# One core, two layers: the weight pieces beside the attention get a tile for their taps, loaded one piece ahead, and a second ring for their rows

## The chip, the core and the metric

The kernel runs on one NeuronCore of a Trainium2 chip. The metric is the device time of one execution in microseconds (us): the median over several executions. The core has five engines that each work through their own list of instructions in order: TensorE (PE in the profile, with its weight loads as PEld), VectorE (DVE), ScalarE (ACT), GpSimd (POOL) and SyncE (SP), which here only issues DMA transfers. They meet at semaphores.

## What is computed

The input is `x`, 4 images of 512 channels by 32 by 32. Two layers follow each other, each with a residual sum. The first is a group norm and a selective-scan (Mamba) layer; it is untouched here. The second, cut to what matters:

```python
x = x + L1(_gn(x))
def L1(x):                                   # per image: 512 channels, 32*32 = 1024 places
    top, center = conv1x1(x, w_top), conv1x1(x, w_center)     # 64 channels each
    bottom = conv3x3(x, w_bottom)                             # 512 channels
    sp = softmax(center.T @ top)                              # over all 1024*1024 entries
    y = (sp @ bottom).reshape(c, h, w)
    return conv3x3(x + y, w_out)
```

All arithmetic is in float32.

## The kernel before

**The two 3x3 convolutions** (`conv3`, lines 1428 to 1524) are done in a transformed form: a convolution's output is put together from 24 products, one for each of six row combinations `p` and four column combinations `q`. So the weights have to be transformed once: from nine taps to 6 x 4 matrices of 512 by 512. These lie in device memory, four tensors `u_b` (for `w_bottom`) and four `u_o` (for `w_out`). For each product `conv3` loads 1 MB of them into a tile `uw` (line 1479, ring `u`, three tiles), issues eight passes of 128x512 matmuls for it (line 1483), and the sums go through DVE and POOL. The inputs of a product come from `spread` (four DVE instructions into a tile `v`, ring `v`, two tiles), which reads a row pair `rr` (`row_pair`, line 1384: a ring `rr` with one single tile). A pair is made from temporaries `e`, `f`, `g`, `h`, `k`, `l` (ring `rt`, four tiles): `e` and `f` start on ACT (line 1393), the rest is POOL work.

**The weight transform** is cut into 16 pieces per weight (128 input channels by 128 output channels, all taps). All of `w_bottom` and the first two pieces of `w_out` are done during the first layer. The other 14 pieces of `w_out` are done in the second layer by `piece` (lines 1400 to 1426), beside the attention of the images 0 and 1, seven each. A piece before the change: load the three tap rows (192 KB each, lines 1408 to 1410) into a tile of the ring `v`, in which six rows stand; combine the taps to rows in place (six DVE instructions, lines 1414 to 1419, 128x384 elements each); combine the columns of all six rows at once into a tile `wo` of the ring `u` (three DVE instructions, lines 1422 to 1424, 128x768 each); store four results of 384 KB, two straight from the tile `w`, two from `wo` (line 1426).

**The order of the second layer** (lines 1604 to 1626). For images 0 and 1: `scores` (the two 1x1 convolutions `pt`, sixteen score matmuls `psc`, each copied from PSUM to `st` by ACT at line 1349, then exponentials), `conv3` with `u_b`, `attend`, and at the end `conv3` with `u_o` for both. `attend` (lines 1526 to 1552) has eight steps. Each is eight accumulating products into a PSUM tile `pat` (line 1533), which DVE then adds to the image `xg` (line 1546). After that of steps 1 to 7 one `piece` is called. PSUM tiles of `pat`, `pt` and `psc` share a ring `ps` of three. `attend` of image 0 is followed by `scores` and `conv3` of image 1, `attend` of image 1 by `conv3` of image 0 with `u_o`, which needs every piece.

The order within each engine is set by a scheduler that sorts the program's instructions by priority as it places them and gives out ring tiles; a tile is given again only when all its readers are through, DMAs too. So the order on an engine isn't exactly that of the text. The order on TensorE is the same before and after the change. On the other engines it moves near the pieces; where the prediction uses such a place it says so.

Of the kernel before, what the change touches and what calls it, by code (L numbers as in the profile page):

```python
# [8 lines left out]
F32 = mybir.dt.float32  # L9
AF = mybir.ActivationFunctionType  # L10
ALU = mybir.AluOpType
# [4 lines left out]
P = 128  # L16
B, C, HH, WW = 4, 512, 32, 32
L = HH * WW
NCC = C // P
# [150 lines left out]
def mamba_then_pab_kernel(  # L170
# [25 lines left out]
    nc = tc.nc  # L196
# [24 lines left out]
    for name, src in (("b", b_bottom), ("o", b_out)):  # L221
        t = cpool.tile([1, C], F32, tag=f"brow_{name}", name=f"brow_{name}")
# [6 lines left out]
    def padded(b, pool, tag):  # L229
# [44 lines left out]
    with ExitStack() as l0:  # L274
# [9 lines left out]
        QC = C // 4  # L284
# [933 lines left out]
        for k in range(NPC + EARLY):  # L1218
            u, src = ((ub, w_bottom), (uo, w_out))[k // NPC]
# [8 lines left out]
        for b in range(B):  # L1228
            at = b * NDC * NS
            for n in range(NDC):  # L1230
# [14 lines left out]
                y = [buf(f"y{j}", [P, NK, P], f"y_{b}_{n}_{j}") for j in range(2)]  # L1245
# [14 lines left out]
    with ExitStack() as l1:  # L1260
# [105 lines left out]
        shape = [P, NCC, TI, WW + 2]  # L1366
# [19 lines left out]
        def first_inputs(name, xg):  # L1386

            r = row_pair(name, 1)
            ts = []
            for n, a in (("e", 2), ("f", 1)):  # L1390
                t = tmp(n, name)
                rows = [xg[:, :, k : k + 4 * TI - 3 : 4, :] for k in (a, a + 2)]
                nc.scalar.activation(t, rows[0], AF.Copy, scale=-4.0)
                nc.gpsimd.tensor_add(t, t, rows[1])
                ts.append(t)
            nc.vector.tensor_add(r[:, 0], *ts)
            nc.vector.tensor_sub(r[:, 1], *ts)
            return spread(name, 1, r)

        def piece(k):  # L1400

            c, part = divmod(k, C // QC)
            cs = slice(part * QC, (part + 1) * QC)
            taps = w_out[c * P : (c + 1) * P, :, cs].rearrange("p (y x) o -> p y x o", y=3)
            t = xp.tile([P, NQ, 2, NCC, P], F32, tag="v", name=f"w_{k}", bufs=2)
            t = t.rearrange("p q n c t -> p (q n c t)").rearrange("p (r o) -> p r o", o=QC)
            g, mid = (t[:, a : a + n].rearrange("p (r x) o -> p r x o", x=3) for a, n in ((0, 3 * NP6), (3 * NP6, 3)))
            nc.sync.dma_start(g[:, 0], taps[:, 0])
            nc.sync.dma_start(g[:, NP6 - 1], taps[:, 2])
            nc.sync.dma_start(mid[:, 0], taps[:, 1])  # L1410
            r = [g[:, n].rearrange("p x o -> p (x o)") for n in range(NP6)]
            m = mid[:, 0].rearrange("p x o -> p (x o)")
            stt, dve = nc.vector.scalar_tensor_tensor, nc.vector
            dve.tensor_add(r[1], r[0], r[5])
            stt(r[3], r[5], 4.0, r[0], ALU.mult, ALU.add)
            dve.tensor_sub(r[2], r[1], m)
            dve.tensor_add(r[1], r[1], m)
            stt(r[4], m, -2.0, r[3], ALU.mult, ALU.add)
            stt(r[3], m, 2.0, r[3], ALU.mult, ALU.add)
            o = fp.tile([P, NCC, C], F32, tag="u", name=f"wo_{k}", bufs=3)  # L1420
            o = o.rearrange("p c o -> p (c o)").rearrange("p (q r o) -> p q r o", o=QC, r=8)[:, :, :NP6]
            dve.tensor_add(o[:, 0], g[:, :, 0], g[:, :, 2])
            dve.tensor_sub(o[:, 1], o[:, 0], g[:, :, 1])
            dve.tensor_add(o[:, 0], o[:, 0], g[:, :, 1])
            for q, part in enumerate((g[:, :, 0], o[:, 0], o[:, 1], g[:, :, 2])):
                nc.sync.dma_start(uo[q].rearrange("n p c o -> p n c o")[:, :, c, cs], part)

        def conv3(name, xg, u, bias, first=None, late=None, mid=None):

# [95 lines left out]

        def attend(b, xg, st, rp, xb, between, also):


            for k in range(NCC * NH):
                j, h = divmod(k, NH)  # L1530
                pt = ps.tile([P, C], F32, tag="ps", name=f"pat_{b}_{j}_{h}")
                for m in range(NMC):
                    nc.tensor.matmul(  # L1533
                        pt, st[m][:, 2 * P * j + h : 2 * P * (j + 1) : 2],
                        xb[m // 2][:, m % 2, :],
                        start=(m == 0), stop=(m == NMC - 1),
                    )
                if k == 0:
                    pz = ps.tile([P, T], F32, tag="ps", name=f"pz_{b}")
                    nc.tensor.matmul(pz[:, 0:1], ones, rp, start=True, stop=True)  # L1540
                    rz = spool.tile([P, 1], F32, tag="rz", name=f"rz_{b}")
                    nc.vector.reciprocal(rz, pz[:, 0:1])
                    for _ in between:
                        pass
                img = xg[:, j, 1 + h * HR : 1 + (h + 1) * HR, 1 : WW + 1]
                nc.vector.scalar_tensor_tensor(
                    img, pt.rearrange("p (h w) -> p h w", w=WW), rz, img,
                    ALU.mult, ALU.add,
                )
                for job in also[k : k + 1]:  # L1550
                    if job is not None:
                        piece(job)

        dst = [out[b].rearrange("(c p) h w -> p c (h w)", p=P) for b in range(B)]

# [47 lines left out]

        left = list(range(EARLY, NPC))
        half = len(left) // 2
        st, rp = scores(0, image[0])
        for a in range(0, B, 2):
            for b in (a, a + 1):
                xb = conv3(f"b{b}", image[b], ub, brow[0])
                also = [None] * (8 - half) + left[b * half : (b + 1) * half] if not a else []  # L1610
                after, v = iter(()), None
                if b == a:
                    after = norm(b + 1)
                    next(after)
# [69 lines left out]
```

## Time and profile before

| | |
|---|---|
| median of 3 runs | 3077.31 us (3075.14 to 3077.47) |
| profiled execution, its own time | 3080.41 us |
| span from first to last instruction in it | 3078.6 us |
| mean granted TensorE clock | 0.967 |
| busy: PE, DVE, ACT, POOL | 89%, 78%, 60%, 66% |
| DMA moved | 610.47 MB, mean 198 GB/s |

The profiled execution is 3.1 us (0.1%) longer than the median, and its own time is 1.8 us longer than its span. Times inside it are counted from the start of the span. The first layer takes the first two thirds; the attention of image 0 stands at about 2120 to 2176 us, that of image 1 at about 2296 to 2351 us. In the rows of the timeline the columns are start, time taken, engine, line and operation, output and inputs, count, and in brackets the idle time just before with what ended it. TensorE runs a float32 product in two passes, so counts of matmuls are twice those of the text.

### The profile page before, as it was taken

How to read it: one execution, taken by the hardware profiler on the slowest of the kernel's cores; microseconds unless marked ns; L12 is line 12 of the kernel's file. 1: busy time of each engine (PE TensorE's matmuls, PEld its weight loads, DVE VectorE, ACT ScalarE, POOL GpSimd, SP SyncE). 2: the span in 40 equal slices, each digit the busy share in tenths (PEclk: the TensorE clock that was granted, in tenths of full speed). 3: DMA queues.
4: the chain of work that ended last, by engine and by line, in shares of the span. 5: the costliest groups of instructions: out<-in, count | busy, mean ns of one | idle time of the engine just before them, and what ended most of it. 6: DMA issues, size and time to landing. Idle time of an engine off the chain costs nothing.

```text
span 3078.6 us, 35834 instructions
## 1 busy us (share of the span) xinstructions
PE 2745.6 (89%) x11512; PEld 1611.2 (52%) x11512; DVE 2395.5 (78%) x3129; ACT 1842.3 (60%) x3179; POOL 2022.4 (66%) x1047
## 2 busy tenths in 40 slices
PE   4789789999889999889999978799895999999998
PEld 2346556666666656556666655544342444444444
DVE  3569999989999989999999999976756475456164
ACT  4579889998789999789999888530210012130000
POOL 7899977899967889967989999743230332233132
PEclk9899899999999999999999999999997999999999
DMA  6766544577734567734667754566776897718397
GB/s 182 205 193 206 167 119 141 166 214 230 223 111 144 165 194 237 234 105 138 176 181 215 220 158 147 134 218 232 232 259 190 290 329 248 286 55 286 126 318 259
DMA packets 408500, 610.47 MB, mean 198 GB/s; under 512 B 46041, under 2 KB 244953, under 8 KB 383737
## 3 DMA queue, kind: packets, MB, share of 16 engines
q1 hardware_dynamic: 399504, 593.66, 61.3%
q10 hardware_dynamic: 8648, 14.26, 1.3%
q8 instruction: 92, 1.51, 0.2%
q14 instruction: 96, 0.78, 0.1%
q0 software_dynamic: 160, 0.26, 0.0%
HBM read 511.09 MB, written 96.99 MB: 198 GB/s over the span
## 4 chain that ended last, share of the span: by engine, by line
PE 42%; DVE 22%; ACT 12%; DMA 5%; issue 5%; POOL 4%; SPq 0%; DVEq 0%; POOLq 0%; ACTq 0%
PE m_b L1483 10%; PE m_o L1483 10%; DVE da L884 7%; PE y L913 4%; PE pat L1533 4%; DVE u L884 3%; ACT sc L844 3%; PE pz L394 2%; DVE dbx L884 2%; PE po L394 2%; PE u L870 2%; ACT da L832 2%; PE psc L1345 2%; ACT u L832 2%; DVE dbx L900 2%
## 5 line engine op out<-in xcount | busy, mean ns | idle before, releaser
L906 POOL TENSOR_TENSOR da<-da,cbc 128x1024 f32<-128x1024 f32 x288 | 680.8, 2369 | 154.6 <-DVE carry_sb L889 63.9
L859 POOL TENSOR_TENSOR dbx<-dtx,bbc 128x1024 f32<-128x1024 f32 x224 | 530.0, 2371 | 59.6 <-PE y L913 32.2
L844 ACT ACTIVATE sc<-dtxt,bt_sb 128x256 f32<-128x256 f32 x1152 | 504.7, 497 | 48.2 <-PE u L870 47.6
L832 ACT ACTIVATE da<-dt,a_sb 128x512 f32<-128x512 f32 x576 | 395.0, 713 | 39.7 <-PE y L913 34.3
L884 DVE TENSOR_TENSOR_SCAN da<-da,carry_sb,u 128x512 f32<-128x512 f32 x288 | 356.0, 1262 | 27.7 <-PE u L870 22.3
L913 PE MATMUL y<-ident,da 128*128 128x128 f32 x2304 | 319.9, 282 | 56.4 <-POOL da L906 52.6
L1483 PE MATMUL m_o<-uw_o,v_o 128*128 128x512 f32 x768 | 337.9, 600 | 35.8 <-DMA uw_o<-u_o 35.8
L870 PE MATMUL u<-ident,sc 128*128 128x128 f32 x2304 | 335.7, 278 | 38.0 <-DVE da L884 28.1
L884 DVE TENSOR_TENSOR_SCAN da<-da,u 128x512 f32<-128x512 f32 x288 | 348.7, 1211 | 3.9 <-PE u L870 3.6
L913 PEld LDWEIGHTS y<-ident,da 128*128 128x128 f32 x2304 | 268.4, 145 | 159.0 <-POOL da L906 107.5
L1483 PE MATMUL m_b<-uw_b,v_b 128*128 128x512 f32 x768 | 336.5, 598 | 7.4 <-DMA uw_b<-u_b 7.4
L870 PEld LDWEIGHTS u<-ident,sc 128*128 128x128 f32 x2304 | 268.5, 143 | 113.9 <-DVE da L884 38.7
L832 ACT ACTIVATE u<-dt,a_sb 128x512 f32<-128x512 f32 x448 | 297.4, 681 | 37.3 <-DVE dbx L900 14.7
L913 PE MATMUL y<-ident,dbx 128*128 128x128 f32 x1792 | 255.8, 281 | 23.8 <-POOL dbx L906 14.0
L394 PE MATMUL pxm<-xt,winc 128*128 128x345 f32 (+3 forms) x704 | 252.5, 501 | 27.3 <-DMA winc<-in_w_in_dram 12.6
L913 PEld LDWEIGHTS y<-ident,dbx 128*128 128x128 f32 x1792 | 209.8, 144 | 100.5 <-issue 32.1
L1483 PEld LDWEIGHTS m_o<-uw_o,v_o 128*128 128x128 f32 x768 | 146.3, 192 | 219.7 <-issue 180.6
L394 PE MATMUL pz<-xt,winc 128*128 128x512 f32 x512 | 242.3, 600 | 11.5 <-ACT sz L707 2.1
L1483 PEld LDWEIGHTS m_b<-uw_b,v_b 128*128 128x128 f32 x768 | 146.1, 191 | 193.5 <-issue 183.4
L906 POOL TENSOR_TENSOR dbx<-dbx,cbc 128x1024 f32<-128x1024 f32 x96 | 227.1, 2366 | 26.1 <-DVE carry_sb L889 17.2
L1533 PE MATMUL pat<-y_b,st 128*128 128x512 f32 x512 | 221.6, 593 | 0.4 <-ACT grstd_l L255 0.4
L394 PEld LDWEIGHTS pxm<-xt,winc 128*128 128x128 f32 x704 | 132.7, 199 | 116.0 <-issue 49.1
(232 smaller groups left out, 4316.8 us busy)
## 6 DMA issues: line engine op xcount, KB each, us to landing
cbc<-bcd SPq DMA_DIRECT2D x512, 256.0 KB, 3.7
uw_b<-u_b SPq DMA_DIRECT2D x96, 1024.0 KB, 4.8
uw_o<-u_o SPq DMA_DIRECT2D x96, 1024.0 KB, 4.8
bbc<-bcd SPq DMA_DIRECT2D x224, 256.0 KB, 3.6
u_b<-work SPq DMA_DIRECT2D x192, 128.0 KB, 2.7
winc<-in_w_in_dram SPq DMA_DIRECT2D x72, 256.0 KB, 3.8
szd<-sz SPq DMA_DIRECT2D x32, 512.0 KB, 3.4
szl<-szd SPq DMA_DIRECT2D x32, 512.0 KB, 4.9
```

What stands on the lines that cost most here:

```text
L394: lambda k=k, lhs=lhs, rhs=rhs: nc.tensor.matmul(p()[:, at : at + cols], lhs(), rhs(), start=(k == 0), stop=(k == n - 1)),
L832: nc.scalar.activation(t, dt()[:, j], AF.Exp, scale=a_sb[:, at : at + 1])
L844: nc.scalar.activation(sc()[:, k], dtxt()[:, k], AF.Copy, scale=bt[:, at, s : s + 1])
L859: lambda: nc.gpsimd.tensor_mul(hc(), dtx(), b_bc().to_broadcast([P, 2, T])),
L870: nc.tensor.transpose(u()[:, k * P : (k + 1) * P], sc()[:, k, j, :], ident)
L884: nc.vector.tensor_tensor_scan(ht, *((hc()[:, j], u()) if on_act else (u(), hc()[:, j])), carry_sb[:, j, s : s + 1] if h else 0.0, ALU.mul ...
L900: lambda j=j, u=u: nc.vector.tensor_mul(hc()[:, j], u(), c_bc()[:, 0]),
L906: lambda: nc.gpsimd.tensor_mul(hc(), hc(), c_bc().to_broadcast([P, 2, T])),
L913: nc.tensor.matmul(y[j]()[:, k, :], hc()[:, j, k * P : (k + 1) * P], ident, start=(s == 0 and k == 0), stop=(s == NS - 1 and k == NK - 1), ...
L1345: nc.tensor.matmul(pt, top[:, m * P : (m + 1) * P], center[:, h * T : (h + 1) * T], start=True, stop=True,)
L1483: nc.tensor.matmul(m[q], v[:, q, k, c, :], w[:, c, :], start=(c == 0), stop=(c == NCC - 1 and not extra),)
L1533: nc.tensor.matmul(pt, st[m][:, 2 * P * j + h : 2 * P * (j + 1) : 2], xb[m // 2][:, m % 2, :], start=(m == 0), stop=(m == NMC - 1),)
```

## The change

`piece` is split in two. `piece_taps` loads the three tap rows into a tile `wt` of the ring `u`. `piece` makes the four middle rows in a tile `wr` of the ring `rr` (the ring of one tile that the row pairs use); the two end rows are the taps themselves and stay in `wt`. The column combinations go to `wo` (ring `u`) in two groups, one from the four rows of `wr` and one from the two end rows of `wt`: six DVE instructions instead of three, with the same elements. The stores are six instead of four: for two of the four results the end rows come from `wt` and the middle rows from `wr`. `attend` loads the taps of the first piece ahead of its first step, and those of each next piece ahead of the work of the one before. The pieces now follow the steps 0 to 6. The tile in the ring `v` is no longer used.

```diff
-        def piece(k):
+        def piece_taps(k):
...
-            t = xp.tile([P, NQ, 2, NCC, P], F32, tag="v", name=f"w_{k}", bufs=2)
...
+            t = fp.tile([P, NCC, C], F32, tag="u", name=f"wt_{k}", bufs=3)
+            t = t.rearrange("p c o -> p (c o)")[:, : 9 * QC].rearrange("p (y x o) -> p y x o", y=3, x=3)
+            for y in (0, 2, 1):
+                nc.sync.dma_start(t[:, y], taps[:, y])
+            return k, t
+
+        def piece(k, t):
...
+            g = tp.tile([P, 2, *shape[1:]], F32, tag="rr", name=f"wr_{k}", bufs=1)
...
-            dve.tensor_add(r[1], r[0], r[5])
-            stt(r[3], r[5], 4.0, r[0], ALU.mult, ALU.add)
-            dve.tensor_sub(r[2], r[1], m)
-            dve.tensor_add(r[1], r[1], m)
-            stt(r[4], m, -2.0, r[3], ALU.mult, ALU.add)
-            stt(r[3], m, 2.0, r[3], ALU.mult, ALU.add)
+            dve.tensor_add(r[0], y0, y2)
+            stt(r[2], y2, 4.0, y0, ALU.mult, ALU.add)
+            dve.tensor_sub(r[1], r[0], y1)
+            dve.tensor_add(r[0], r[0], y1)
+            stt(r[3], y1, -2.0, r[2], ALU.mult, ALU.add)
+            stt(r[2], y1, 2.0, r[2], ALU.mult, ALU.add)
             o = fp.tile([P, NCC, C], F32, tag="u", name=f"wo_{k}", bufs=3)
...
-            dve.tensor_add(o[:, 0], g[:, :, 0], g[:, :, 2])
-            dve.tensor_sub(o[:, 1], o[:, 0], g[:, :, 1])
-            dve.tensor_add(o[:, 0], o[:, 0], g[:, :, 1])
-            for q, part in enumerate((g[:, :, 0], o[:, 0], o[:, 1], g[:, :, 2])):
-                nc.sync.dma_start(uo[q].rearrange("n p c o -> p n c o")[:, :, c, cs], part)
+            for w, src in ((o[:, :, 1 : NP6 - 1], g), (o[:, :, 0 : NP6 : NP6 - 1], t[:, 0:3:2])):
+                dve.tensor_add(w[:, 0], src[:, :, 0], src[:, :, 2])
+                dve.tensor_sub(w[:, 1], w[:, 0], src[:, :, 1])
+                dve.tensor_add(w[:, 0], w[:, 0], src[:, :, 1])
+            for q, x in ((0, 0), (3, 2)):
+                nc.sync.dma_start(dst[q][:, 0 : NP6 : NP6 - 1], t[:, 0:3:2, x])
+                nc.sync.dma_start(dst[q][:, 1 : NP6 - 1], g[:, :, x])
+            for q in (1, 2):
+                nc.sync.dma_start(dst[q], o[:, q - 1])
...
         def attend(b, xg, st, rp, xb, between, also):
 
+            ahead = piece_taps(also[0]) if also else None
...
-                for job in also[k : k + 1]:
-                    if job is not None:
-                        piece(job)
+                if also:
+                    taps = piece_taps(also[k + 1]) if k + 1 < len(also) else None
+                    piece(*ahead)
+                    ahead = taps
...
-                also = [None] * (8 - half) + left[b * half : (b + 1) * half] if not a else []
+                also = left[b * half : (b + 1) * half] if not a else []
```

Three moves follow from it in the scheduler's order. On ACT, the start of `e` for the next convolution (line 1393, `e_o`) stands ahead of the first copy of a score product in `scores` of image 1, and that of `f_o` behind the second; before, they stood behind the seventh and the tenth. On DVE, the row pair `rr_b` of image 1 (lines 1396 and 1397) stands behind the last piece of image 0's attention instead of amid the pieces, and the row pair of rows 3 and 4 for the convolution `o` of image 0 (line 1449) behind the last piece of image 1's attention instead of ahead of the first.

More of the change, by code (lines that the diff above doesn't have):

```diff
@@ L1404, in piece @@
             taps = w_out[c * P : (c + 1) * P, :, cs].rearrange("p (y x) o -> p y x o", y=3)
-            t = xp.tile([P, NQ, 2, NCC, P], F32, tag="v", name=f"w_{k}", bufs=2)
[L1406 to L1410, printed above, removed]
@@ L1411, in piece @@
-            r = [g[:, n].rearrange("p x o -> p (x o)") for n in range(NP6)]
-            m = mid[:, 0].rearrange("p x o -> p (x o)")
-            stt, dve = nc.vector.scalar_tensor_tensor, nc.vector
-            dve.tensor_add(r[1], r[0], r[5])
-            stt(r[3], r[5], 4.0, r[0], ALU.mult, ALU.add)
-            dve.tensor_sub(r[2], r[1], m)
-            dve.tensor_add(r[1], r[1], m)
-            stt(r[4], m, -2.0, r[3], ALU.mult, ALU.add)
-            stt(r[3], m, 2.0, r[3], ALU.mult, ALU.add)
+            t = fp.tile([P, NCC, C], F32, tag="u", name=f"wt_{k}", bufs=3)
@@ new lines, in piece_taps @@
+            t = t.rearrange("p c o -> p (c o)")[:, : 9 * QC].rearrange("p (y x o) -> p y x o", y=3, x=3)
[3 more added lines that the diff above has]
+        def piece(k, t):
+            c, part = divmod(k, C // QC)
+            cs = slice(part * QC, (part + 1) * QC)
+            dst = [u.rearrange("n p c o -> p n c o")[:, :, c, cs] for u in uo]
+            g = tp.tile([P, 2, *shape[1:]], F32, tag="rr", name=f"wr_{k}", bufs=1)
+            g = g.rearrange("p n c i x -> p (n c i x)")[:, : 12 * QC].rearrange("p (r x o) -> p r x o", r=4, x=3)
+            y0, y1, y2 = (t[:, y].rearrange("p x o -> p (x o)") for y in range(3))
+            r = [g[:, n].rearrange("p x o -> p (x o)") for n in range(4)]
+            stt, dve = nc.vector.scalar_tensor_tensor, nc.vector
+            dve.tensor_add(r[0], y0, y2)
[4 more added lines that the diff above has]
+            stt(r[2], y1, 2.0, r[2], ALU.mult, ALU.add)
@@ L1549, in attend @@
                 )
-                for job in also[k : k + 1]:
-                    if job is not None:
-                        piece(job)
+                if also:
+                    taps = piece_taps(also[k + 1]) if k + 1 < len(also) else None
+                    piece(*ahead)
+                    ahead = taps
+                    if taps is None:
+                        also = []
         dst = [out[b].rearrange("(c p) h w -> p c (h w)", p=P) for b in range(B)]
```

## Prediction

> **What bounds the kernel now.** I looked first where TensorE idles in the second layer, since it is busy 89% of the span and its order is the same after the change: the timeline of TensorE, from the attention of image 0 to the end.
>
> ```profile
> 2128.16 48.34 PE L1533 MATMUL pat<-y_b,st 128*128 128x512 f32 x112 [0.35 <-ACT grstd_l L255]
> 2176.34 3.61 PE L1324 MATMUL pt<-xg,wt_sb 128*128 128x512 f32 x8
> 2185.76 6.14 PE L1324 MATMUL pt<-xg,wt_sb 128*128 128x512 f32 x8 [5.81 <-DVE xg L1546]
> 2196.15 3.75 PE L1483 MATMUL m_b<-uw_b,v_b 128*128 128x512 f32 x4 [4.25 <-DMA uw_b<-u_b]
> 2199.69 14.52 PE L1345 MATMUL psc<-center,top 128*128 128x512 f32 x32
> ...
> 2302.99 48.32 PE L1533 MATMUL pat<-y_b,st 128*128 128x512 f32 x112
> 2386.06 10.11 PE L1483 MATMUL m_o<-uw_o,v_o 128*128 128x512 f32 x16 [34.76 <-DMA uw_o<-u_o]
> ...
> 2734.28 7.06 PE L1324 MATMUL pt<-xg,wt_sb 128*128 128x512 f32 x16
> ...
> 2742.89 13.90 PE L1345 MATMUL psc<-center,top 128*128 128x512 f32 x32
> ...
> 2893.72 7.03 PE L1483 MATMUL m_o<-uw_o,v_o 128*128 128x512 f32 x16
> ```
>
> Image 1's attention ends at 2351.3 and TensorE then waits 34.76 us, because convolution `o` may not load weights before all pieces are stored. Without pieces (image 3) the same place has no wait: 2893.72. After image 0's attention the way to the first `psc` is 2199.69 - 2176.34 = 23.35 us; without pieces (image 2) it is 2742.89 - 2734.28 = 8.61. The first 16 matmuls after the long wait take 10.11 us instead of 7.03.
>
> Then the waits by engine between 2296 and 2390, the chain of waits there, and the DMA view of 2299 to 2371:
>
> ```profile
> DVE w L1414 <- DMA w<-in_w_out_dram: 33.3, 7, 5.9
> ```
>
> ```profile
> 2314.34 0.56 DVE w L1419
> 2315.32 3.78 DMA u_o<-w
> 2319.59 4.09 DMA w<-in_w_out_dram
> 2323.81 0.47 DVE w L1414
> ```
>
> ```profile
> GB/s 72 0 164 286 286 253 212 0 0 182 285 284 242 209 0 22 286 280 259 277 78 0 162 288 285 241 226 0 0 281 282 281 258 104 0 94 280 288 242 284
> ```
>
> A piece is a closed loop: rows, store, wait for landing, load, wait for landing. The first rows start at 2299.50, 2311.33, 2323.81, 2335.50, 2347.37, 2359.36, 2371.11: 11.9 us each, 83 us for seven beside 55 us of attention. DMA alternates between nothing and 286 GB/s, its ceiling with these packets of some 500 bytes.
>
> **Part 1: taps of their own, one ahead.** In the new SP order the taps of piece k+1 stand ahead of the stores of piece k, so the 4.09 us of load leave the loop. What paces it now? Three rows:
> - DVE: six row instructions start 0.47 us apart (2.8 us). Of the column instructions, 768 elements take 0.87 us and 384 take 0.47, so 0.07 is fixed; three times (512 + 256 elements) give 2.8, and some 0.3 more where each waits for the one before. With one `xg` (0.66): 6.6 us. The three instructions added cost 0.2 a piece, covered if another term is larger, else 14 x 0.2 = 3 us.
> - The ring of one: the next piece's rows may not start before the stores from `wr` have landed: rows 2.8, with image 0 an `xg` between them (0.66), one store issued ahead 0.5, landing 3.6 (median for 384 KB, 2.8 to 4.4): 6.9 to 7.6 us, 7.1 where I need one value.
> - Bytes: 3 x 192 KB + 1536 KB of stores are 2.163 MB; at 286 GB/s 7.56 us.
>
> The largest is 7.55, my cadence C. Both ends: no less than 6.9, the distance of two `pat` steps (DVE must follow them); 9.2 where pieces already overlapped (image 0's pieces, about 2149 to 2195 for five, with two tiles). SP issues nine transfers a piece, 9 x 0.5 = 4.5 us, and the store of `wt`'s end rows, with the stores of `wo` behind it, waits for taps issued 3 us earlier: inside the 7.55.
>
> **Part 2: the end of image 1's attention**, on the clock of before. Piece one's taps take the tile of a weight that TensorE releases 6.8 us before the convolution ends (two products of 3.4), so its rows run beside the tail. `wo` must wait for the last weight tile, 2296.0; with DVE's `n_b` and the columns it is done at 2300.1; piece two starts about 2301.2, the last at 2301.2 + 5 x 7.55 = 2339.0. Add 6.4 for rows, `xg` and columns (2345.4), 2.6 until the store that the first weight load waits for has landed (it is issued one column group earlier), and 6.4 for that load (2379.64 issued, 2386.06 used before): 2354.4. The attention ends at 2351.3, so the wait is 3.1 us: **31.7 saved**. The row pair moved behind the last piece (two of 1.29 us, four of `spread`) is needed 27 us into the convolution and is hidden by its first eight products.
>
> The windows of the granted clock price the slow start:
>
> ```profile
> 2386.00:2388.00 2.00, 1.94 (x3) 0.91 (x4) 0.00 (x0) 0.52 (x1) 2.00 (x2) 0.50 1.01 426
> 2388.00:2390.00 2.00, 2.00 (x4) 0.95 (x3) 0.00 (x0) 0.00 (x0) 2.00 (x1) 0.50 0.78 324
> 2390.00:2392.00 2.00, 2.00 (x3) 0.68 (x2) 0.00 (x0) 0.00 (x0) 2.00 (x2) 0.50 0.02 8
> 2392.00:2394.00 2.00, 2.00 (x6) 0.90 (x5) 0.00 (x0) 0.60 (x1) 2.00 (x2) 0.98 0.28 45
> ```
>
> The clock (third number from the end) is 0.50 for 6.1 us, 10.11 - 7.03 = 3.1 us lost. A wait of 3 us may or may not drop it (one of 4.25 did, at 2196); I take half, **1.5 saved**. The Trainium skill ("TensorE: Matmul & The Clock Gate", Part 1) has half rate until a busy window of about 3.4 us; by it an estimate of the loss is 1.7, not 3.1, and the sum would be 0.7 us less. The row decides.
>
> **Part 3: the end of image 0's attention.** Here the pieces meet POOL, which runs four adds from 2132.72 to 2143.6:
>
> ```profile
> 2135.22 3.01 POOL L1394 TENSOR_TENSOR e_b<-e_b,xg 128x1088 f32<-128x1088 f32 x1
> ```
>
> ```profile
> 2136.00 2.64 DVE L1414 TENSOR_TENSOR w<-w 128x384 f32<-128x384 f32 x1
> 2138.57 2.65 DVE L1415 SCALAR_TENSOR_TENSOR w<-w 128x384 f32<-128x384 f32 x1
> ```
>
> A DVE instruction of 0.54 takes 2.64 while POOL adds: about one gets through per POOL instruction. The Trainium skill ("SBUF — State Buffer", "SBUF: two separate sides") says the pair of ports that both share is locked for a whole instruction; the trace agrees. So four of the second piece's six column instructions pass until 2143.6, the rest by 2145; then 4 x 7.55 to the last piece, 2175.2; its `wr` has landed at 2182.3.
>
> Only then may DVE make `rr_b`, which was done amid the pieces before. Behind it, in DVE's new order: two `rr_b` (2.4), `xg` (0.66), four `spread` (4.56), `xg` (0.66), two `rr_b` (2.4), four `spread` (4.56), the first of two more `rr_b` (1.2): 16.4 us. POOL's `l_b` and `k_b`, which wait for `rr_b` and ran at 2154 before, now run here: 2 x 2.54 locked, 21.5 in all, to 2203.8. That last instruction frees the tile of `e_o`, and `e_o` now stands **ahead of all sixteen copies of scores on ACT**. TensorE can fill the three tiles of `ps` and then waits for ACT; behind the waiting `psc` on its queue stand all products of the convolution. `e_o` 1.05 and one copy 0.6: the fourth `psc` at 2205.5; thirteen at 0.86, and 0.1 left of `f_o`'s 1.05, as ACT gains 0.27 a copy: 2216.8. TensorE has then been idle some 9 us (its third `psc` has its tile about 2195) and the clock is low: between 0.6 (14.52 - 13.90) and 3.1, I take 2.5: 2219.3. Before, `psc` ended at 2199.69 + 14.52 = 2214.2: **5.1 lost**. The waits at 2185 and 2196 go, and a longer one comes behind them.
>
> **Sum.** -31.7 - 1.5 + 5.1 = -28.1. The profiled execution took 3080.41, so 3052.3 there; the median is 3.1 lower, so 3077.3 - 28.1 = **3049.2 us**. With the cadence as variable: the wait in Part 2 is 5C - 34.7, the loss in Part 3 is 4C - 25.1.
>
> **Rivals.**
> - *Longer cadence.* Loads, stores and the ring get in each other's way, as with image 0 before, C = 9.2: the wait is 11.3 (23.5 saved, no clock gain), the loss 11.7: 3065.5. For it: SP's in-order waits. Against it: 286 GB/s is held slice after slice. Chance 17%.
> - *Slower: the ring of one closes the loop again.* If `wr`'s landing takes the place of the tap load, because its store queues behind `wo` and the next taps, C stays near 11.9: the wait is 24.8 (10.0 saved), the loss 22.5, so 12.5 slower: 3089.8. It decides from 34.76 - (5C - 34.7) = 4C - 25.1, C = 10.5. A store would have to land 7 us after issue; the longest of the 56 took 4.4. Chance 7%.
> - *No block in `scores`.* If `e_o`'s tile comes free in time, image 0's end looks like image 2's, 8.61 instead of 23.35 and 13.9 instead of 14.5: 15.4 saved instead of 5.1 lost, 3028.7. Against it: DVE's sixteen microseconds are in its order. Chance 8%.
> - *The change doesn't do what it says*: the ring `u` of three, shared with the weights and `wo`, holds the next taps back, the loop is as before: 3077. Against it: the SP order. Chance 4%.
>
> **Numbers.** The forecast has 64%; its own range is C from 6.9 (no wait, with the clock 37.9 saved, 2.5 lost: 3041.9) to 8.3 (28.0 and 8.1: 3057.4). To hold 8 in 10 the range reaches over most of the longer cadence and part of the way to the unblocked case: 3034 to 3067. Faster than 3071 (0.2%, what a measurement here can tell): 64 + 17 + 8, less 2 for the far end of the long cadence, 87%; the same 6%; slower 7%.
>
> **What would show it.** Right: first rows of successive pieces 7 to 8 us apart; DMA near 280 GB/s without empty slices from 2301 to 2350; the first `m_o` 2 to 5 us behind the last `pat`; on ACT, `e_o` waiting for `rr_b` and TensorE idle 7 us or more inside `psc`. Wrong: rows 9 us or more apart, waiting for `wr`'s stores; `psc` ending sooner after the attention than 38 us; a clock of 1.00 through `psc`.

## The result, and the profile after

The changed kernel takes 3051.73 us (median of four runs, 3048.10 to 3055.46) against 3077.39 for the kernel before, measured beside it (four runs, 3075.14 to 3079.36): a ratio of 0.9915, 95% interval 0.9899 to 0.9931. It is 25.7 us faster; 28.1 were forecast, and the time lies 2.5 us above the predicted one.

The profiled execution took 3048.93 us, span 3047.1. TensorE's timeline, as it was read before (start, time taken, engine, line and operation, count, idle time just before and what ended it):

```profile
2113.74 7.12 PE L1546 MATMUL pat<-y_b,st 128*128 128x512 f32 x16
2122.73 48.34 PE L1546 MATMUL pat<-y_b,st 128*128 128x512 f32 x112 [1.53 <-DVE rz L1555]
2170.91 3.61 PE L1324 MATMUL pt<-xg,wt_sb 128*128 128x512 f32 x8
2176.76 3.71 PE L1324 MATMUL pt<-xg,wt_sb 128*128 128x512 f32 x8 [2.24 <-DVE xg L1559]
2180.31 1.88 PE L1494 MATMUL m_b<-uw_b,v_b 128*128 128x512 f32 x4
2188.05 5.36 PE L1345 MATMUL psc<-center,top 128*128 128x512 f32 x6 [5.86 <-DVE xg L1559]
2198.03 14.08 PE L1345 MATMUL psc<-center,top 128*128 128x512 f32 x26 [4.62 <-ACT st L1349]
...
2295.46 7.03 PE L1546 MATMUL pat<-y_b,st 128*128 128x512 f32 x16
...
2302.46 48.32 PE L1546 MATMUL pat<-y_b,st 128*128 128x512 f32 x112
2353.83 8.70 PE L1494 MATMUL m_o<-uw_o,v_o 128*128 128x512 f32 x16 [3.05 <-DMA uw_o<-u_o]
```

Three places are to be seen. The wait behind image 1's attention is 3.05 us instead of 34.76. The scores of image 0, which ran in one go of 14.52 us, are now torn: TensorE stands 5.86 us ahead of them and 4.62 inside. And the first `m_o` still run below full speed, 8.70 us instead of 7.03.

The piece is no longer a closed loop. The DMA view of the time between the first rows of the second and of the last piece of image 1 (2301.1 to 2339.3):

```profile
GB/s 251 298 236 267 276 330 345 311 293 284 220 282 302 331 336 173 271 298 225 285 278 322 342 314 316 300 224 327 300 342 317 112 284 288 210 300 218 329 341 325
...
q1 hardware_dynamic: 21952, 10.88, 100.7%
```

The slices of nothing are gone, and the packets of the queue now fill the sixteen DMA engines (100.7% of their time; 64.8% before, in 2311.3 to 2371.1). The mean is 285 GB/s, where it was 181.

To compare kernels I cut the second layer at four events of TensorE's timeline: the first `pat` of image 0, the end of its scores (the last `psc`), the first `pat` of image 1, and the first `m_o`. "Pace" is the mean distance of the first rows of image 1's second to last piece (of the third to last in e12, whose second piece stands right behind the first and whose third comes 13.3 us later). Times in us, from one profile each; the ratio is to the kernel before on the same chip.

| kernel | ratio (95%) | pat to psc's end | to pat of image 1 | to m_o | to the end | pace |
|---|---|---|---|---|---|---|
| before | 1 | 93.9 | 81.8 | 90.1 | 692.5 | 12.0 |
| after | 0.9915 (0.9899, 0.9931) | 98.4 | 83.4 | 58.4 | 693.3 | 7.6 |
| after, again (e11) | 0.9908 (0.9884, 0.9931) | 98.4 | 81.8 | 58.1 | 694.1 | 7.7 |
| e1 no load ahead | 0.9978 (0.9966, 0.9989) | 90.9 | 83.5 | 77.7 | 698.5 | 11.5 |
| e2 old tiles, load ahead | 1.0003 (0.9991, 1.0015) | 92.4 | 81.8 | 89.0 | 692.6 | 11.9 |
| e3 rows in ring v | 0.9938 (0.9922, 0.9954) | 95.6 | 81.8 | 60.9 | 693.1 | 7.7 |
| e4 e_o on DVE | 0.9885 (0.9867, 0.9903) | 91.0 | 81.8 | 58.1 | 689.6 | 7.6 |
| e5 e4 and xg first | 0.9861 (0.9847, 0.9876) | 82.3 | 81.8 | 58.1 | 691.9 | 7.6 |
| e6 xg first alone | 0.9886 (0.9871, 0.9901) | 82.7 | 89.4 | 58.1 | 689.2 | 7.7 |
| e7 one store less | one run | 97.1 | 81.8 | 55.2 | 690.4 | 6.9 |
| e8 before, earlier step | 0.9998 (0.9986, 1.0010) | 92.5 | 81.8 | 89.3 | 695.2 | 11.9 |
| e9 l_b, k_b on DVE | 0.9903 (0.9885, 0.9920) | 93.3 | 81.8 | 58.4 | 690.5 | 7.7 |
| e10 e5, six pieces | 0.9880 (0.9863, 0.9897) | 82.5 | 81.8 | 55.2 | 695.2 | 7.5 |
| e12 rows in two rings | 0.9916 (0.9891, 0.9942) | 98.6 | 81.8 | 60.1 | 692.1 | 7.3 |

From the first `pat` to the end of the span, before takes 958.3 us and after 933.4, 24.9 less, close to the 25.7 between the medians. The work behind the first `m_o` is the same in all of them and takes 689 to 699 us, so a difference of a few us there is not assigned to any edit. The scheduler orders each variant anew, and `e_o` does not stand at the same place on ACT in all of them: it is ahead of all sixteen score copies in after, e11 and e3, behind one in e7, behind three in e9, behind thirteen in e6 and behind all in e1; in e12 it is ahead even of the second half of `center` and `top`.

### The profile page after: what moved, and what is told of

Same layout as the page of the kernel before. It is cut to its first block, busy times and chain, and to the rows that moved or that the text cites. A ratio compares the mean times of both kernels' runs of the same rounds, so it can differ in the third digit from the quotient of the medians.

```text
span 3047.1 us, 35912 instructions
## 1 busy us (share of the span) xinstructions
PE 2742.4 (90%) x11512; PEld 1607.5 (53%) x11512; DVE 2402.3 (79%) x3171; ACT 1842.4 (60%) x3179; POOL 2022.1 (66%) x1047
## 4 chain that ended last, share of the span: by engine, by line
PE 45%; DVE 23%; ACT 16%; DMA 6%; issue 5%; POOL 4%; SPq 1%; ACTq 0%; DVEq 0%; POOLq 0%
PE m_o L1494 10%; PE m_b L1494 9%; DVE da L884 7%; PE y L913 5%; PE pz L394 4%; ACT sc L844 4%; PE pat L1546 4%; DVE u L884 3%; ACT da L832 3%; PE po L394 2%; PE u L870 2%; ACT u L832 2%; DVE dbx L884 2%; PE pxm L394 2%; PE psc L1345 2%
## 5 line engine op out<-in xcount | busy, mean ns | idle before, releaser
L870 PE MATMUL u<-ident,sc 128*128 128x128 f32 x2304 | 336.1, 278 | 35.3 <-DVE da L884 24.9
```

What stands on the lines that cost most here:

```text
L870: nc.tensor.transpose(u()[:, k * P : (k + 1) * P], sc()[:, k, j, :], ident)
```

## The experiments

**Which part opened the loop: e1, e2, e8.** The change loads ahead, has tiles of its own, and starts at step 0. Each was tried without the others, or the others without it.

```diff
-            ahead = piece_taps(also[0]) if also else None
+            ahead = None
...
-                    taps = piece_taps(also[k + 1]) if k + 1 < len(also) else None
-                    piece(*ahead)
-                    ahead = taps
...
+                    piece(*piece_taps(also[0]))
+                    also = also[1:]
```

> The changed kernel, but each piece issues its own three tap loads at its own start, behind the stores of the piece before. Theory (the load that leaves the loop is the gain): the first rows of image 1's pieces stand 10.5 to 12 us apart instead of 7.6, the wait ahead of the first m_o is 18 to 26 us instead of 3.1, and the time is 3070 to 3092 us. Rival (the weight tiles of their own and the ring are the gain, the order of the load is not): 7.6 us apart, a wait of 3 us, 3050 to 3056 us.

Measured: 3071.70 us, a pace of 11.5 and a wait of 22.4 ahead of the first `m_o`. The theory holds in all three numbers. Without the load ahead only 0.2% is left of the whole. At the place itself more is left: the stretch from image 1's first `pat` to `m_o` is 12.4 us shorter than before (77.7 against 90.1), 6.9 of it by the earlier first rows (see e8); what e1 then takes behind `m_o`, 698.5, is the longest of all.

e2 is the kernel before, its piece cut behind the tap loads, and the loads of the next piece called ahead of the arithmetic of this one:

```diff
+            jobs = [j for j in also if j is not None]
+            ahead = piece_taps(jobs[0]) if jobs else None
...
-                        piece(job)
+                    taps = piece_taps(jobs[1]) if len(jobs) > 1 else None
+                    piece(*ahead)
+                    ahead, jobs = taps, jobs[1:]
```

> The kernel before with its 18-row tile in the ring of two, its four stores and its pieces at steps 1 to 7, and one edit: the loads of the next piece are issued ahead of the arithmetic and stores of this one. Theory (load ahead is the gain, and two old tiles are nearly enough for it): rows 8 to 9.5 us apart instead of 11.9, the wait ahead of the first m_o 10 to 20 us instead of 34.8, 3055 to 3066 us. Rival (the old tile is held until its stores land, so a load ahead needs tiles of its own): 11 to 12 us apart, a wait over 28 us, 3071 to 3079 us.

Measured: 3078.69 us, ratio 1.0003: nothing at all. My theory fell, the rival held. The waits by engine (engine, waiting tile and line, what it waits for: us in total, times, longest) between 2290 and 2385 have the row of the kernel before again (33.3 us there), and the chain of waits shows the same loop:

```profile
DVE w L1420 <- DMA w<-in_w_out_dram: 33.1, 7, 5.8
```

```profile
2310.84 3.79 DMA u_o<-w
...
2315.11 4.02 DMA w<-in_w_out_dram
...
2319.26 0.56 DVE w L1420
```

The store of a piece lands (2310.84 + 3.79), and only then is the load of the *next* piece issued, although its call stands earlier. A ring of two should let it go. But in image 1's attention the second tile of ring `v` holds the input of the coming convolution `o` (`v_o`, written from 2264.8 on and read by `m_o` from 2380.5 on), so the pieces had one tile between them. A load ahead needs a tile that is free; the order of the calls alone does nothing.

e8 is the kernel before with the pieces after steps 0 to 6:

```diff
-                also = [None] * (8 - half) + left[b * half : (b + 1) * half] if not a else []
+                also = left[b * half : (b + 1) * half] if not a else []
```

> The kernel before with one edit: the pieces run after steps 0 to 6 of each attention instead of 1 to 7, loads, tiles and stores as before. Theory (an earlier start saves its own distance and no more): rows still 11.9 us apart, but the first of them 6 to 7 us earlier, so a wait of 27 to 29 us ahead of the first m_o instead of 34.8, and 3067 to 3072 us. Rival (the loads already go out at the same time, and only the program order changes): wait over 33 us, 3075 to 3079 us.

Measured: 3079.00 us, ratio 0.9998, a wait of 34.0; the first rows come 3.9 us behind image 1's first `pat`, before it was 3.5. The rival held. The seven us by which the changed kernel starts earlier (first rows 3.3 us *ahead* of the first `pat`, in e1 3.4 ahead) come with the tap tile in the ring `u`: the old tile had to wait for ring `v`, where the input of convolution `b` was still being read. In e8 the first load is issued at 2290.26, 0.2 us behind the first `pat` and so behind the end of that convolution; in after at 2288.78, 6.7 us ahead of the first `pat`.

**What sets 7.6 us: e3, e7, e12.**

```diff
-            g = tp.tile([P, 2, *shape[1:]], F32, tag="rr", name=f"wr_{k}", bufs=1)
+            g = xp.tile([P, NQ, 2, NCC, P], F32, tag="v", name=f"wr_{k}", bufs=2)
```

> The changed kernel with the four computed rows (wr) in the ring of two 16 KB tiles that the change left free, instead of the ring of one of the row pairs. Two questions. What sets 7.6 us between image 1's pieces: by theory the bytes (2.16 MB at 286 GB/s), and it stays 7.4 to 7.7 with a wait of 2 to 3.5 us ahead of the first m_o; by the rival the ring of one (DVE's waits for landed wr stores), and it falls to 6.6 to 7.0 with a wait under 1 us. What delays image 0's scores: by theory rr_b, which no longer waits for the last wr store and so is ready early, with rt free and e_o not held; the 13.9 us wait of e_o falls under 3 us and the last psc ends 5 to 9 us earlier, 3040 to 3047 us in all. Rival (DVE's own queue of pieces holds the scores, whichever ring is used): psc within 1.5 us, 3048 to 3055 us.

Measured: 3056.34 us, pace 7.7, wait 5.5 ahead of `m_o`; the scores of image 0 end 2.8 us earlier than in after. This seemed to speak for the bytes, but by e2's finding the ring of two had one tile to give here as well, so on the pace it decides nothing. Its first rows come 0.8 us behind image 1's first `pat` instead of 3.3 ahead, which the wait shows. And the scores of image 0 did not come free: `e_o` still waited 8.1 us for `rr_b`, as DVE began its last column operation 66.5 us behind the first `pat`; in after even `rr_b`, behind all columns, begins at 61.0. My expectation for image 0 missed.

```diff
-            for q in (1, 2):
-                nc.sync.dma_start(dst[q], o[:, q - 1])
+            nc.sync.dma_start(dst[1], o[:, 0])
...
```

e7 leaves out the store of one of a piece's four results, so only the pieces' distances are read from it.

> The changed kernel without the store of wo for q = 2 in the fourteen pieces of the two attentions (6 of a piece's 33 row-and-column blocks: 0.39 of 2.16 MB). That part of u_o is filled with other data by stores beside image 0's first convolution, so the second convolution computes with wrong weights and only the distances of the pieces are to be read, not the total. Theory (bytes at 286 GB/s set the pace): 1.77 MB need 6.2 us, so the pieces of image 1 come 6.6 to 7.1 us apart (VectorE's work or the ring of one are next), and the wait ahead of m_o is under 1 us. Rival (the landing time of the wr stores sets it, whatever the bytes): 7.4 to 7.7 us apart.

Measured: rows 7.22, 6.73, 6.93, 6.78 and 6.99 us apart, no wait ahead of `m_o`. With 18% fewer bytes the DMA engines are no longer full (2307.2 to 2341.8):

```profile
GB/s 0 236 210 320 327 329 324 285 16 257 211 271 323 323 309 288 91 288 205 332 233 343 309 294 65 291 191 285 284 339 317 290 95 284 210 229 281 325 301 297
...
q1 hardware_dynamic: 17836, 8.81, 90.4%
```

Slices of 16, 91, 65 and 95 GB/s are back, one per piece. The pace fell to 6.9, into the range of the two other terms (6.6 and 7.1), as the theory had it. But fewer bytes also land sooner, so a true second tile was tried:

```diff
-            g = tp.tile([P, 2, *shape[1:]], F32, tag="rr", name=f"wr_{k}", bufs=1)
+            if k % 2:
+                g = xp.tile([P, NQ, 2, NCC, P], F32, tag="v", name=f"wr_{k}", bufs=2)
...
+            else:
+                g = tp.tile([P, 2, *shape[1:]], F32, tag="rr", name=f"wr_{k}", bufs=1)
...
```

> The changed kernel with the four computed rows (wr) of every second piece in a tile of the ring v and of the others in the ring rr as before. In e3 the ring of two had only one tile to give in image 1's attention, since v_o of the next convolution held the other, so e3 did not try two tiles there; this does. Theory (bytes set the pace of 7.6 us): the pieces still come 7.4 to 7.7 us apart, with the DMA engines busy over 95%, and the wait ahead of the first m_o stays 2.5 to 3.1 us; from the first pat to the end 929 to 935 us. Rival (the landing of the wr stores in the ring of one sets it, and e7 gained because fewer bytes landed sooner): VectorE no longer waits for wr stores, 6.6 to 7.0 us apart, no wait ahead of m_o, 3 to 5 us less.

Measured: 3054.63 us; no wait of DVE for a `wr` store is left between 2285 and 2372, and from the third piece to the last (2312.72 to 2341.76) the pace is 7.26, between the two expectations. The DMA engines are full:

```profile
q1 hardware_dynamic: 17052, 8.45, 102.2%
```

At their 291 GB/s a piece's 2.16 MB need 7.4. So full DMA engines are the bound, and of after's 7.6 us the ring of one costs at most 0.4 a piece. The whole gained nothing: the second piece's rows stood behind the first's, both late (first rows 2.6 us behind the `pat`), and the wait became 4.7.

**What tears image 0's scores: e4, e5, e6, e9.**

```diff
-                nc.scalar.activation(t, rows[0], AF.Copy, scale=-4.0)
-                nc.gpsimd.tensor_add(t, t, rows[1])
+                if name == "o0":
+                    for c in range(NCC):
+                        nc.vector.scalar_tensor_tensor(t[:, c], rows[0][:, c], -4.0, rows[1][:, c], ALU.mult, ALU.add)
...
```

> The changed kernel with e_o and f_o of image 0 made on VectorE (eight small multiply-adds of one channel block each) instead of two ScalarE copies and two GpSimd additions, so that nothing that waits for rr_b stands ahead of the score copies on ScalarE. Theory (the score copies stood behind e_o): the 4.6 us wait of psc for st goes below 1 us, the last psc ends 4 to 7 us earlier, 3044 to 3050 us. Rival (VectorE is the bound there: the 5.9 us wait for xg stays and the eight added operations of some 0.5 us each come on top): psc at the same time or up to 3 us later, 3050 to 3057 us.

Measured: 3040.02 us, the scores end 7.4 us earlier, and the wait inside them is gone:

```profile
2192.76 16.37 PE L1345 MATMUL psc<-center,top 128*128 128x512 f32 x32 [5.86 <-DVE xg L1563]
```

With the wait of 4.62 went what it had cost the clock (the scores took 5.36 + 14.08 in after and 16.37 here, 3.1 us less at work). The time lies below the 3044 to 3050 of the theory, but not by the scores alone: of the 13.0 us that e4 is shorter than after from the first `pat` on, 7.4 stand here, 1.6 in the convolution, where after waits for a weight, and 3.7 lie behind `m_o`, where nothing is assigned. The wait ahead of the scores stayed to the hundredth. In e5 and e6 the second half of `rr_b` (and so `v_b` behind it) was made to follow image 0's last `xg` on DVE; e5 has e4's edit too, e6 has it not.

```diff
-            nc.vector.tensor_sub(r[:, 1], *ts)
+            i = nc.vector.tensor_sub(r[:, 1], *ts)
+            if name == "b1":
+                tc.add_manual_dep(i.ins, held[0].ins.name, mybir.DependencyInfo(mybir.DependencyClass.NoSync, mybir.DependencyReason.DATA), reason="order")
...
-                nc.vector.scalar_tensor_tensor(
+                held[b] = nc.vector.scalar_tensor_tensor(
```

> The kernel of e4 (e_o and f_o of image 0 on VectorE), and one order more: the last update of image 0 (xg from the last pat, which frees the PSUM bank that the scores need) goes ahead of the second half of rr_b and of the v_b operations on VectorE, instead of behind them. Theory (in e4 what is left is the 5.9 us in which psc waits for that xg, at 2191.87 though its pat ended at 2179): this wait falls below 1.5 us, the last psc ends 5 to 7 us earlier than in e4 counted from the first pat (91.0 us there), 3032 to 3036 us. Rival (v_b is what the next convolution waits for, so that what psc gains m_b loses): 3038 to 3042 us, with a new wait ahead of m_b.

> The changed kernel with only the order of e5 (last xg of image 0 ahead of v_b), e_o and f_o again on ScalarE. Theory (two blocks in series, and the later one, the score copies behind e_o, which waits for rr_b at about 2196, decides): psc starts earlier but stands longer for its copies, the last psc moves by less than 2 us, 3049 to 3054 us. Rival (the blocks add up independently, as the two waits of 5.9 and 4.6 us suggest): 5 to 6 us earlier, 3044 to 3047 us.

Measured: e5 3037.29 us, ratio 0.9861 (0.9847 to 0.9876); the time lies between the theory's range and the rival's, and no new wait came ahead of `m_b`. No wait is left between the second `pt` and the end of the scores, and they run at the time of an undisturbed image:

```profile
2191.74 13.90 PE L1345 MATMUL psc<-center,top 128*128 128x512 f32 x32
```

They end 8.7 us earlier than in e4, more than the 5 to 7 expected: the wait of 5.86 had also cost the clock, 16.37 - 13.90 = 2.5 us. The two were timed on different chips, so the ratios are to be compared, not the medians: 0.9885 and 0.9861 are 7 us apart, and the time behind the first `pat` fell by 6.4 (920.4 to 914.0). By its ratio this version is the fastest that I ran, though the intervals of e4, e6 and e10 overlap with its own.

e6, 3044.59 us, was expected to gain nothing, and gained: the scores end at 82.7. It does not try the order of `xg` alone, though, because the scheduler also moved `e_o` on ACT, from ahead of all sixteen copies to behind thirteen of them. So TensorE gets through the scores, and what `e_o` holds up moved on. Rows of ACT, of TensorE and of GpSimd:

```profile
2203.67 0.58 ACT L1349 COPY st<-psc 128x512 f32<-128x512 f32 x1 [0.27 <-PE psc L1345]
2212.37 1.11 ACT L1395 ACTIVATE e_o<-xg 128x1088 f32<-128x1088 f32 x1 [8.11 <-DVE rr_b L1473]
```

```profile
2241.48 54.28 PE L1498 MATMUL m_b<-uw_b,v_b 128*128 128x512 f32 x120 [4.84 <-ACT e_b L1506]
```

```profile
2221.77 2.28 POOL L1396 TENSOR_TENSOR f_o<-f_o,xg 128x1088 f32<-128x1088 f32 x1
2231.13 0.38 POOL L1355 PARTITION_ALL_REDUCE ma<-mp  x1 [7.08 <-issue]
```

GpSimd's half of `e_o` and three more such operations, which begin when ACT's half is done, run from 2213.6 to 2224.0, and its maximum for the softmax (`ma`) stands behind them: its input is ready at 2217 in both kernels, but it runs at 2216.9 in e5 and at 2231.1 in e6. Only half of this delay is the queue. From 2224.0 on GpSimd stands idle for 7.08 us, and the profile shows nothing that it waits for; e9 has 5.82 and before 9.40 of the same ahead of `ma`, and e5 has 7.40 between `ma` and its next operation. What fills this time no run here shows. ACT's exponentials wait for `ma`, and `e_b`, which TensorE needs, stands behind them on ACT. So 7.6 us of the 15.7 are given back in the convolution. Neither of my pictures describes this: the block of `e_o` was neither added nor hidden, it came at a later place. How much the order of `xg` is worth with `e_o` left ahead of the copies no run shows.

```diff
-                nc.gpsimd.tensor_sub(l, rows(0), rows(2))
-                nc.gpsimd.tensor_sub(k, rows(5), rows(3))
+                eng = nc.vector if name == "b1" else nc.gpsimd
+                eng.tensor_sub(l, rows(0), rows(2))
+                eng.tensor_sub(k, rows(5), rows(3))
```

> The changed kernel with l_b and k_b of image 1's first convolution subtracted on VectorE instead of GpSimd, where they ran beside v_b. Theory (the two v_b operations of 3.55 us were 1.22 us operations that GpSimd's l_b and k_b held up): the four v_b take 4 times 1.2 us, so the last xg of image 0 comes 4.7 us earlier, and its wait of 5.9 us ahead of psc falls to about 1; rr_b, with two more operations of 1.2 to 1.3 us on VectorE, ends 2 us earlier, and with it the first e_o; the last psc ends 2 to 4 us earlier than 98.2 us after the first pat. Rival (the two v_b are long of themselves, or for a port that e_o or the DMAs use): they stay at 3.5 us, rr_b ends 2.6 us later, and the last psc 2 to 3 us later.

Measured: 3046.85 us, the scores end 5.1 us earlier. Rows of DVE, first of after, then of e9:

```profile
2179.08 3.55 DVE L1375 TENSOR_TENSOR v_b<-rr_b 128x1024 f32<-128x1024 f32 x1
2182.55 3.55 DVE L1376 TENSOR_TENSOR v_b<-rr_b 128x1024 f32<-128x1024 f32 x1
```

```profile
2187.32 1.22 DVE L1375 TENSOR_TENSOR v_b<-rr_b 128x1024 f32<-128x1024 f32 x1
2188.46 1.22 DVE L1376 TENSOR_TENSOR v_b<-rr_b 128x1024 f32<-128x1024 f32 x1
```

The same instruction takes a third of the time when GpSimd is not subtracting beside it, so the theory holds that GpSimd held it up, and the gain is a little above its 2 to 4 us. The wait ahead of the scores is gone; the one inside is 6.5 us, since the scores begin sooner while `e_o` begins only 2.6 us earlier (80.1 us behind the first `pat`, 82.7 in after). Here too the scheduler moved `e_o`, behind three copies, so the 5.1 us are not the price of the two long `v_b` alone.

**One piece less beside image 1: e10.** Edits to e5:

```diff
-    NP6, NQ, EARLY = 6, 4, 2
+    NP6, NQ, EARLY = 6, 4, 3
...
-                also = left[b * half : (b + 1) * half] if not a else []
+                also = (left[: half + 1], left[half + 1 :])[b] if not a else []
```

> The kernel of e5, with one of u_o's pieces more made in the first layer (3 instead of 2, its arithmetic on GpSimd there), so that image 1's attention has six pieces instead of seven. Theory (with a pace of 7.6 us the last store then lands some 5 us ahead of the end of the attention): no wait ahead of the first m_o, instead of 2.7 us; its first 16 run at full clock, 7.1 us instead of 8.8; from image 1's first pat to the end 3 to 4.5 us less than e5's 750.0, the first layer as before, so 3033 to 3035 us. Rival (the first layer has no room for a piece more and gives it back): a first pat of image 0 more than 4 us later than in the other kernels, 3037 to 3045 us.

Measured: 3039.39 us, ratio 0.9880, not better than e5. Up to the first `m_o` the theory holds to the decimal: no wait, 55.2 instead of 58.1, the first sixteen in 7.03 us, and the first layer had room (first `pat` at 2122.84, e5 2123.36). The time lies in the range of the rival, but the rival's reason did not come. From image 1's first `pat` to the end e10 takes 750.4 us, e5 750.0: all of it is given back behind. Two waits for weights in image 2's first convolution are 3.7 us, and the second costs 1.7 more at work (15.67 where 13.97 is usual for 32):

```profile
2612.20 7.11 PE L1502 MATMUL m_b<-uw_b,v_b 128*128 128x512 f32 x16 [1.29 <-DMA uw_b<-u_b]
2621.74 15.67 PE L1502 MATMUL m_b<-uw_b,v_b 128*128 128x512 f32 x32 [2.43 <-DMA uw_b<-u_b]
```

Such waits also came and went in kernels that are alike there (2.0 and 2.1 us in e1 and e8, 0.73 and 0.55 in e5), so whether this is chance or the price of the edit stays open.

**The scatter: e11.**

> The changed kernel once more, untouched, beside e9 and e10. The four runs it was timed with stood at 3048 to 3049 and at 3054 to 3055 us. If its time is one value with a scatter that comes from the first layer (its first pat stood at 2113.7 us there and at 2115.8 to 2123.5 in the profiles of nine other kernels whose first layer is the same), the time from the first pat to the end is 933 within 1.5 us again, while the first pat moves by several us; the median is 3049 to 3056. Rival (the scatter comes from the pieces): the time behind the first pat differs by over 3 us.

Measured: four runs from 3041.61 to 3057.02, median 3046.59. The profiled one took 3057.02, 8 us more than the first profile, and yet its time behind the first `pat` is 932.4, the first profile's 933.4. The difference is the first `pat`: 2122.33 against 2113.74. So the theory of the scatter holds, as far as two profiles show it: it sits in the first layer, which none of these edits but e10's touches. The median lies 2.4 us below the 3049 to 3056 that I expected. Over the fourteen profiles the first `pat` stands between 2113.7 and 2123.5, and a gain of 3 us is better read behind it than from medians.

## Why the prediction was right, and where not

- **Pace (Part 1): right, and in the main for the reason given.** 7.55 forecast from the bytes, 7.6 measured, DMA full (after), 7.3 with two tiles (e12), 6.9 with fewer bytes (e7). The term of the ring, 7.1, was close behind, as e7 shows. The 286 GB/s of the forecast are no ceiling, though: slices of up to 345 GB/s stand beside slices of 112 in after, and only their mean, 285, is the same. That is luck in the decimals.
- **"The load leaves the loop" (Part 1): right as a fact, short as a reason.** I gave it to the SP order alone. e2 has that order and no gain, e1 has the tiles, a pace of 11.5 and 0.2%; the short pace needs both, because the old ring had one free tile. The same missing sight made me expect 8 to 9.5 us of e2.
- **End of image 1's attention (Part 2): right.** Wait 3.1 forecast, 3.05 measured; 31.7 us saved forecast, 90.08 - 58.37 = 31.7 measured. The early first piece came by the ring `u`, as written; the step it is called after plays no part (e8). The last decimal is luck: the last piece began 0.8 us later than forecast (43.8 us behind the first `pat` instead of 43.0), and what follows it took 0.8 less (14.6 instead of 15.4).
- **Slow clock (Part 2): right in size, by luck in the single case.** 1.5 forecast as half of 3.1; 10.11 - 8.70 = 1.4 measured. It is in truth one of two outcomes: the same kernel in e11 waited 2.72 us and kept the full clock (7.13). The 3.1 of before was one outcome too, since e8 lost only 1.8 behind a wait of nearly the same length (33.96 us, first sixteen in 8.79). The windows of after, with the clock as third number from the end:

```profile
2353.80:2355.80 2.00, 1.97 (x3) 0.94 (x4) 2.00 (x3) 0.00 (x0) 0.00 (x0) 0.50 0.98 414
2355.80:2357.80 2.00, 2.00 (x5) 0.92 (x4) 0.69 (x2) 1.21 (x2) 1.23 (x1) 0.69 0.78 324
```

- **End of image 0's attention (Part 3): right in the chain that ends last and in its size, not in where TensorE waits.** From the first `rr_b` to `e_o`, 21.5 us forecast and 2196.39 - 2174.75 = 21.6 measured; from `e_o` to the end of the scores 15.5 and 15.7; the end of the scores 5.1 later forecast, 98.4 - 93.9 = 4.5 measured. On ACT it reads as foretold:

```profile
2196.39 1.11 ACT L1393 ACTIVATE e_o<-xg 128x1088 f32<-128x1088 f32 x1 [13.94 <-DVE rr_b L1469]
2197.41 1.05 ACT L1349 COPY st<-psc 128x512 f32<-128x512 f32 x2
```

  One sign of being right did not come: 7 us or more of idle time inside `psc` were foretold, 4.62 were measured. TensorE waited elsewhere: 2.24 us ahead of the second `pt`, though this wait was to go, and 5.86 ahead of the scores, which I had only as a late third tile. The latter is a block of its own that decides once `e_o` is gone: e4 takes `e_o` away and gains 7.4, the order of `xg` on top gains 8.7 more. And 1.2 of the 4.5 us stand ahead of the first `pt`, where the second group of `pat` waits 1.53 us (for DVE's `rz`) instead of 0.35; the forecast has no such term.
- **Sum.** Forecast -28.1; the profiles give +4.5 and -31.7, +1.6 ahead of image 1's attention (a wait of 1.30 us for a weight, absent in e11), -1.4 for the clock, and +2.1 behind, inside the scatter: -24.9. No term of the forecast is off by more than 0.6 us; what was not in it is no larger than what comes and goes between profiles that are alike there. That the clock's term came out is the luck told above.
- **Rivals.** A longer pace, the ring closing the loop and "does nothing" did not come. The unblocked case did not come by itself, but e5 nearly brings it: 11.6 us saved at this place against before (82.3 instead of 93.9), where 15.4 were worked out for image 2's 8.61 us from `pt` to `psc`; in e5 it is 11.25, with one wait of 2.4 left for `xg`.

## What to carry to other kernels

A load called one piece ahead is ahead only if its tile is free: count who else holds the ring in that stage before trusting its number of buffers. When a loop opens, look for what it now ends on (here the bytes) and for the small instruction that the new order puts at the head of an in-order queue: here two of them cost 16 us, half of what the open loop gained, and busy times show neither. An edit under a scheduler can move other instructions too, as e6 and e9 show, so read the order on each queue before the result is put down to the edit. If the common part of a program scatters by more than the effect, cut the profile at an event behind that part.

## What the runs showed of the hardware

- The transfers of this stage, 10.89 MB in 21,954 packets of 0.5 KB each, fill the sixteen DMA engines at 285 to 291 GB/s (after, e12); while the weights of the first `m_o` are loaded, the window shows 414 GB/s (after, 2353.80 to 2355.80).
- The clock behind a short wait of TensorE: after 3.05 us (after), 3.04 (e9) and 2.72 (e5) the granted clock began at 0.50 to 0.65 and the first sixteen matmuls took 8.7 to 8.8 us; after 2.75 (e4, e6) and 2.72 (e11) it stayed at 1.00 and they took 7.1. Shorter waits show the same. Ahead of the second `pt`, 2.19 us in e9 were followed by a clock of 0.58 and 5.40 us for eight matmuls, 2.24 us in after by 1.00 and 3.71:

```profile
2185.00 5.40 PE L1324 MATMUL pt<-xg,wt_sb 128*128 128x512 f32 x8 [2.19 <-DVE xg L1560]
```

  So between 2 and 3 us the length of the wait does not decide, and what does no run here shows. The loss does not follow the length either: it was 1.7 behind 3.05 us (after), 3.15 behind 4.73 (e12), 1.8 behind 33.96 (e8) and 3.1 behind 34.76 (before). The loss of 1.7 to 1.8 us agrees with the estimate of 1.7 that the prediction worked out from the Trainium skill ("TensorE: Matmul & The Clock Gate", Part 1); the 3.1 does not. The same part of the Trainium skill has an idle window of some 3.4 us before the clock falls, which is longer than the waits of 2.19 to 3.05 us that cost it here.
- A DVE instruction with two inputs in SBUF takes 3.55 us instead of 1.22 beside GpSimd's subtractions (after, e9). The subtractions come out longer too: `l_b` takes 3.50 us there, the same subtraction of the next convolution (`l_o`) 2.53 (after). The Trainium skill ("SBUF — State Buffer", "SBUF: two separate sides") has the port pair that both share locked for a whole instruction, and these rows agree.
